# A recurrent layer on one core: one product cut into four column tiles, and three conv parts moved past a stage's end

## The chip, the cores and the metric

The kernel runs on one core of a Trainium2 chip. The metric is the device time of one execution in microseconds (us), as the median of several runs. The core's engines work in parallel, each through its own queue in order: TensorE (PE; its weight loads are shown apart as PEld), VectorE (DVE), ScalarE (ACT), GpSimd (POOL) and SyncE (SP), which issues the transfers here. They wait for each other through semaphores.

## The reference

The input `x` has 16 rows of 256 x 512 fp32 values; the condition has 512 values per row. Four layers follow each other, each added to `x`:

```python
x = x + _L0_cond_ref(x, cond_2048, L0_cond_Wq, L0_cond_Wo)          # masked self-attention
x = x + _L1_cond_ref(x, cond_2048[:, None, :])                      # causal conv, 16 taps, over the 256 positions
x = x + _L2_cond_ref(cond_2048, x, L2_cond_W_ih, L2_cond_W_hh, L2_cond_b_ih, L2_cond_b_hh)   # GRU over 256 steps
x = x + _L3_cond_ref(x, cond_2048, L3_cond_Wq, L3_cond_Wk, L3_cond_Wv, L3_cond_b)            # masked attention
```

The third layer is the one that the change touches. Its cell, run over 256 steps for 16 rows with a state of 512 values:

```python
gi = x @ W_ih + b_ih
gh = h @ W_hh + b_hh
r = sigmoid(i_r + h_r); z = sigmoid(i_z + h_z); n = tanh(i_n + r * h_n)
h_new = (1.0 - z) * n + z * h
```

## The kernel before

The kernel has three stages. The first (to about 667 us) computes the first attention for one row after another, in an order that a planner works out from durations and due times; its path for these inputs is `attend0_together`. As soon as a row is ready in `xT` (features on partitions), `early` (L537) makes the conv's first four parts of 16 positions for that row: on VectorE a product of a sliding view with the taps (L546), a sum over the taps (L547) and an addition of `x` (L548), three operations for each part, after one POOL copy of 64 positions into the small tile `early` (L540). The parts land in `yw[0]` (parts 1 and 2) and `yw[1]` (parts 3 and 4). There is a third such tile, `yw[2]`, made for the recurrence; the first thing written into it is a conv of step 0.

The second stage (to about 1796 us) is the recurrence. Here the order of every engine's work is written out by hand. The 16 rows stand as the 32 columns of a stationary operand (two steps' worth), and weights stream past. Each product's output is cut into four column tiles: four matmuls of 32 stationary columns each, that write 32 output partitions each (`state_part`, L1064, for the state's parts of r, n and z; `input_part`, L1043, for the inputs' parts of r and z). The inputs' part of n is made otherwise, by `turned_part` (L1051): weights are stationary, 128 columns of them in one matmul, and 16 steps of inputs (256 columns) stream past. It takes 16 such matmuls for the 16 steps of a part p; the recurrence does one in each step, for the part that follows, and every fourth one is followed by a ScalarE operation (L1062) that adds the bias and moves the result from PSUM into `turned`.

A step (`step`, L1078) is a loop through three engines. PE does r, n and z with the state; ScalarE takes the sigmoid of r (L1092); VectorE transposes r and n (L1093, L1095), multiplies and adds (L1096, L1097); ScalarE takes the tanh (L1099); VectorE transposes z (L1100), ScalarE its sigmoid (L1101), and VectorE ends with `d`, `m` and the new state, written to `hist` (L1102 to L1104). The next step's r needs that state. Behind each step, the loop body puts, in this order: input parts of a later step on PE; on odd steps three ScalarE copies of the biases (L1136); one `turned_part`; in some steps a ScalarE copy of conv results (`take`, L1035); and two pieces of VectorE work, conv operations (L528) or additions of the state to `xT` (`add_part`, L1071). The product with `turned_part` is in steps 0 to 239; steps 240 to 255 have none, and steps 254 and 255 have no input parts either.

Ahead of step 0 stand: ScalarE's loading of its function table (L1113), products that place the biases in PSUM (L1116), their copies (L1118), `take` for part 0, all input parts of the first two steps, and the 16 matmuls of `turned_part` for part 0. Before them in the program, outside of the order by hand, two POOL memsets clear `hist` and VectorE copies the condition into it as the first state (L1017 to L1019). The third stage is the second attention.

Of the kernel before, what the change touches and what calls it, by code (L numbers as in the profile page):

```python
# [15 lines left out]
P = 128  # L16
NEG = -1e30
B, D, T = 16, 256, 512
# [7 lines left out]
TAPS = 16  # L26
WIN = 32
PART = 16
EARLY = 4
# [231 lines left out]
def tile_kernel(ctx: ExitStack, tc: tile.TileContext, x, cond, Wq0, Wo0, W_ih, W_hh, b_ih, b_hh,  # L261
                Wq3, Wk3, Wv3, b3, consts, out, cols):
    nc = tc.nc
    inp = x
    KC = D // P
    NT = T // P
# [12 lines left out]
    condT = cpool.tile([P, NT, B], F32, tag="condT", name="condT")  # L279
# [7 lines left out]
    xT = cpool.tile([P, NT, B, D], F32, tag="xT", name="xT")  # L287
# [5 lines left out]
    yw = [ypool.tile([P, NT, B, WIN], F32, tag=f"yw{i}", name=f"yw{i}") for i in range(2)]  # L293
# [6 lines left out]
    wih = cpool.tile([P, NT, 3 * T], F32, tag="wih", name="wih")  # L300
# [236 lines left out]
    def early(b, w, xs, products):  # L537

        if w == 0:
            yield "POOL", 0.7, lambda: nc.gpsimd.tensor_copy(xs[:, :, TAPS - 1 :], xT[:, :, b, 0 : EARLY * PART])  # L540
        a = xs[:, :, w * PART : w * PART + TAPS].unsqueeze(2).broadcast_to([P, NT, PART, TAPS])
        steps = [list(d) for d in a.ap]
        steps[2][0] = 1
        every = bass.AP(tensor=a.tensor, offset=a.offset, ap=steps)
        y = yw[w // 2][:, :, b, w % 2 * PART : (w % 2 + 1) * PART]
        yield "DVE", 1.3, lambda: nc.vector.tensor_tensor(products, every, condT.unsqueeze(2).broadcast_to([P, NT, PART, TAPS]), ALU.mult)  # L546
        yield "DVE", 1.3, lambda: nc.vector.tensor_reduce(y, products, AX.X, ALU.add)  # L547
        yield "DVE", 0.2, lambda: nc.vector.tensor_tensor(y, y, xs[:, :, TAPS - 1 + w * PART : TAPS - 1 + (w + 1) * PART], ALU.add)  # L548
# [5 lines left out]
    with tc.tile_pool(name="setup0", bufs=1) as sp, tc.tile_pool(name="psetup0", bufs=2, space=PSUM) as pss:  # L554
# [23 lines left out]
        ps = pss.tile([P, T], F32, tag="psm", name="pgood")  # L578
# [3 lines left out]
        for j in range(NT):  # L582
            ps = pss.tile([P, T], F32, tag="psm", name=f"condT{j}")
# [4 lines left out]
        ps = pss.tile([P, T], F32, tag="psm", name="places")  # L588
# [27 lines left out]
    def attend0_all():  # L616
        with ExitStack() as es:
# [55 lines left out]
            def finish0(b, j):  # L673
                ps = at.small(f"po0_{b}_{j}")
                for g in range(at.G):
                    nc.tensor.matmul(ps[:, 0:D], lhsT=at.avs[b * at.G + g][:, j * P : (j + 1) * P], rhs=woP[:, g, :],
                                     start=(g == 0), stop=False)
                for dc in range(KC):
                    nc.tensor.matmul(ps[:, dc * P : (dc + 1) * P], lhsT=xs[b][:, dc, j * P : (j + 1) * P], rhs=ident,
                                     start=False, stop=(dc == KC - 1))  # L680
                nc.scalar.copy(xT[:, j, b], ps[:, 0:D])
                if j == NT - 1:
                    for w in range(EARLY):
                        for _, _, f in early(b, w, *tiles):
                            f()

# [20 lines left out]
    def attend0_together():  # L707
# [7 lines left out]
        with ExitStack() as es:  # L715
# [202 lines left out]
            def finish(b, g0, x, cx, done):  # L918

                oc, gt, po = ocs.new(), gts.new(), pss.new()  # L920
                n = plan.add("SP", 3.0, g0 + 0.3, [pss.take(po)], lambda: nc.sync.dma_start(
                    out=PO[po.i], in_=places_dram[b : b + 1, :].broadcast_to([P, T])))
                for c in range(NK):
                    n = plan.add("DVE", 0.6, g0 + 0.6, [n] + ([gts.take(gt)] if c == 0 else []), lambda c=c: nc.vector.tensor_scalar(
                        GT[gt.i][:, c], PO[po.i], cst("place")[:, c : c + 1], None, ALU.is_equal))
                pss.free(po, n)
                made = []
                for part in range(2):
                    sm = banks.new()

                    def product(part=part, sm=sm):
                        for c in range(2) if part == 0 else [2]:
                            r = P if c < 2 else TAILK + 1
                            for g in range(GQ):
                                nc.tensor.matmul(SM[0:r, sm.i][:, (c % 2) * D : (c % 2 + 1) * D], lhsT=CX[cx.i][:, g, c * P : c * P + r],
                                                 rhs=woT[:, g, :], start=(g == 0), stop=(g == GQ - 1))
                    m = plan.add("PE", 1.72 if part == 0 else 0.87, g0 + 2.2 + 0.05 * part, done + [banks.take(sm)] + ([] if part else [ocs.take(oc)]) + made, product)
                    c = plan.add("ACT", 0.62 if part == 0 else 0.4, g0 + 2.2, [m], lambda part=part, sm=sm: nc.scalar.copy(
                        OC[oc.i][:, 0:2].rearrange("p c d -> p (c d)") if part == 0 else OC[oc.i][0 : TAILK + 1, 2],
                        SM[0 : P if part == 0 else TAILK + 1, sm.i][:, 0 : (2 - part) * D]))  # L940
                    banks.free(sm, c)
                    made.append(c)
                cs.free(cx, m)
                outs, moved = [], []
                for half in range(2):
                    sm = banks.new()

                    def product(half=half, sm=sm):
                        for tj in range(2 * half, 2 * half + 2):
                            dst = SM[:, sm.i][:, (tj % 2) * D : (tj % 2 + 1) * D]  # L950
                            for c in range(NK):
                                r = P if c < 2 else TAILK + 1
                                nc.tensor.matmul(dst, lhsT=GT[gt.i][0:r, c, tj * P : (tj + 1) * P], rhs=OC[oc.i][0:r, c], start=(c == 0), stop=False)  # L953
                            for dc in range(KC):
                                nc.tensor.matmul(dst[:, dc * P : (dc + 1) * P], lhsT=X[x.i][:, dc, tj * P : (tj + 1) * P], rhs=ident,
                                                 start=False, stop=(dc == KC - 1))
                    m = plan.add("PE", 3.45, g0 + 2.4 + 0.05 * half, made + [n, banks.take(sm)] + moved, product)
                    moved.append(m)
                    outs.append(plan.add("ACT", 0.65, g0 + 2.4, [m], lambda half=half, sm=sm: nc.scalar.copy(
                        xT[:, 2 * half : 2 * half + 2, b], SM[:, sm.i].rearrange("p (c d) -> p c d", d=D))))  # L960
                    banks.free(sm, outs[-1])
                ocs.free(oc, *moved)
                gts.free(gt, *moved)
                xs_.free(x, *moved)
                ea, n = ears.new(), None
                for w in range(EARLY):
                    for engine, dur, f in early(b, w, *ear):
                        n = plan.add(engine, dur, g0 + 3.2 + 0.3 * w, [n] if n else outs + [ears.take(ea)], f)
                ears.free(ea, n)
# [37 lines left out]
    with ExitStack() as es:  # L1007
# [6 lines left out]


        hist = [gw.tile([P, PART, NT, 2 * B], F32, tag=f"hist{i}", name=f"hist{i}") for i in range(2)]
        for t in hist:  # L1017
            nc.gpsimd.memset(t, 0.0)
        nc.vector.tensor_copy(hist[1][:, PART - 1, :, 0:B], condT)  # L1019

        def state(t):

# [28 lines left out]
        def turned_part(p, q):  # L1051

            fo, kc = divmod(q, NT)
            if q == 0:
                turned[p] = gp.tile([P, NT, PART, B], F32, tag="turned", name=f"turned_{p}")
            if kc == 0:
                turned["ps"] = psw.tile([P, T], F32, tag="psm", name=f"pt_{p}_{fo}")
            ps = turned["ps"][:, 0 : PART * B]
            nc.tensor.matmul(ps, lhsT=wih[:, kc, 2 * T + fo * P : 2 * T + (fo + 1) * P],  # L1059
                             rhs=parts[p][:, kc].rearrange("p s b -> p (s b)"), start=(kc == 0), stop=(kc == NT - 1))  # L1060
            if kc == NT - 1:
                nc.scalar.activation(turned[p][:, fo].rearrange("p s b -> p (s b)"), ps, AF.Identity, bias=nbias[:, fo : fo + 1])  # L1062

# [44 lines left out]

        taps = [(f, k, w * WIN) for w in range(EARLY // 2, D // WIN) for f in range(NT) for k in range(TAPS)]
        parts, turned, added = {}, {}, 0  # L1110
        with tc.manual_schedule(engines=ENG):

            nc.scalar.activation(gp.tile([P, NT], F32, tag="table", name="table", bufs=1), nbias, AF.Sigmoid)  # L1113
            for k in range(2):
                for ps, base in zip(sets[k], (0, 32, 64)):
                    nc.tensor.matmul(ps, lhsT=cst("gsel")[base : base + 8], rhs=gbias[base : base + 8], start=True, stop=True)  # L1116
# [425 lines left out]
```

## Time and profile before

| what | us |
|---|---|
| median of three runs (2829.16 to 2835.69) | 2830.13 |
| the profiled execution's own time | 2828.66 |
| its span, from the first instruction to the last | 2826.9 |
| TensorE busy in it | 2747.6 |
| VectorE busy in it | 1845.0 |
| ScalarE busy in it | 1026.1 |
| GpSimd busy in it | 229.4 |

A reader of such a page should keep apart how long an engine is busy and how much of the end it decides. The page's groups give, for each line of the program, an operation with its shapes, how often it came, its total busy time and the mean length of one in ns, and then the idle time of its engine just before. The timeline gives single instructions (or runs of like ones) with start and length in us. A matmul's end is modelled and overlaps the next one's start, so for TensorE the distance from one start of weight loads to the next is the better measure. One fp32 matmul of the program shows as two records on PE and two on PEld.

### The profile page before, as it was taken

Reading aid. Unit: us, or ns where it says so; the run is one execution under the profiler, and the core shown is the slowest. Engines: PE = TensorE matmul, PEld = TensorE weight load, DVE = VectorE, ACT = ScalarE, POOL = GpSimd, SP = SyncE. Lnnn points to the kernel's source line nnn. Section 1 sums busy time; section 2 is a strip of 40 time slices with the busy share of each in tenths; the row PEclk is TensorE's granted clock in tenths of the full one; section 3 lists DMA queues with packets and bytes.
Section 4 is the critical chain, followed back from the end, with each engine's and each line's share of the span. In section 5 each row is a group of like instructions: output and inputs, shape, how many; then the busy total and the mean of one; then the engine's idle time right before and its main releaser. Section 6 shows DMA issues by size and latency. Waiting matters only on the chain.

```text
span 2826.9 us, 99913 instructions
## 1 busy us (share of the span) xinstructions
PE 2747.6 (97%) x45574; PEld 1833.1 (65%) x45574; DVE 1845.0 (65%) x3929; ACT 1026.1 (36%) x2360; POOL 229.4 (8%) x282
## 2 busy tenths in 40 slices
PE   8999999997999999999999999799999999999998
PEld 5666666665888888888888888544444444444442
DVE  3666766675788888888888655565555556555553
ACT  2333333332333333333333332144444444444444
POOL 1010001000000000000000000002111111121112
PEclk9999999998999999999999999999999999999998
DMA  1000000002000000000000000000000000000000
GB/s 61 23 24 12 23 23 24 22 10 99 4 4 4 4 4 4 4 4 4 4 4 4 4 4 4 2 1 12 13 8 8 8 9 8 9 16 8 9 9 17
DMA packets 15370, 36.79 MB, mean 13 GB/s; under 512 B 2084, under 2 KB 3364, under 8 KB 14804
## 3 DMA queue, kind: packets, MB, share of 16 engines
q1 hardware_dynamic: 14932, 30.24, 3.1%
q8 instruction: 361, 5.91, 0.9%
q14 instruction: 77, 0.63, 0.1%
HBM read 21.78 MB, written 8.45 MB: 11 GB/s over the span
## 4 chain that ended last, share of the span: by engine, by line
PE 95%; DVE 3%; ACT 1%; issue 1%; POOL 0%; DMA 0%; SPq 0%; DVEq 0%; ACTq 0%; POOLq 0%
PE pr L1068 9%; PE pn L1068 8%; PE pz L1068 8%; PE sC L1426 7%; PE sC L1380 6%; PE pt L1059 6%; PE avC L1440 5%; PE smA L875 4%; PE smA L901 4%; PE pz L1048 4%; PE pr L1048 4%; PE smC L1346 4%; PE smA L953 3%; PE smC L1288 3%; PE smA L794 3%; PE sC L1386 2%
## 5 line engine op out<-in xcount | busy, mean ns | idle before, releaser
L1395 DVE TENSOR_REDUCE nmC<-sC 128x4 f32<-128x1024 f32 x256 | 301.8, 1221 | 215.5 <-PE sC L1380 209.2
L1433 ACT ACTIVATE wih<-sC 128x1024 f32<-128x1024 f32 x320 | 310.2, 1023 | 177.9 <-PE sC L1426 176.7
L1068 PE MATMUL pr<-whh,hist 128*32 128x128 f32 x8192 | 279.1, 276 | 9.1 <-DVE hist L1104 9.1
L528 DVE SCALAR_TENSOR_TENSOR yw<-xT,condT,yw 128x512 f32<-128x512 f32 x360 | 269.5, 749 | 6.8
L1068 PE MATMUL pn<-whh,hist 128*32 128x128 f32 x8192 | 272.3, 273 | 0.0
L1068 PE MATMUL pz<-whh,hist 128*32 128x128 f32 x8192 | 271.8, 273 | 0.0
L1068 PEld LDWEIGHTS pr<-whh,hist 128*32 128x32 f32 x8192 | 209.5, 110 | 93.7 <-DVE hist L1104 42.3
L1068 PEld LDWEIGHTS pn<-whh,hist 128*32 128x32 f32 x8192 | 230.7, 110 | 0.1
L1068 PEld LDWEIGHTS pz<-whh,hist 128*32 128x32 f32 x8192 | 230.1, 110 | 0.0
L1048 PE MATMUL pr<-wih,xw 128*32 128x128 f32 x4096 | 209.7, 274 | 13.3 <-ACT xw L1041 13.2
L1426 PE MATMUL sC<-qC,kC 32*128 32x512 f32 (+1 forms) x1280 | 219.2, 637 | 0.6 <-ACT wih L1433 0.3
L1048 PE MATMUL pz<-wih,xw 128*32 128x128 f32 x4096 | 210.5, 274 | 0.3 <-issue 0.3
L848 DVE TENSOR_REDUCE whh<-smA 128x2 f32<-128x640 f32 (+1 forms) x192 | 148.9, 817 | 89.4 <-PE smA L840 81.0
L1099 ACT ACTIVATE nn<-pre 128x64 f32<-128x64 f32 x256 | 65.8, 257 | 383.2 <-DVE pre L1097 383.2
L1092 ACT ACTIVATE r<-pr 128x128 f32<-128x128 f32 x256 | 71.1, 278 | 334.7 <-PE pr L1068 334.7
L1059 PE MATMUL pt<-xw,wih 128*128 128x256 f32 x512 | 174.9, 428 | 0.0
L1093 DVE STREAM_TRANSPOSE rT<-r 128x128 f32<-128x128 f32 x256 | 79.7, 311 | 145.7 <-ACT r L1092 145.3
L1380 PE MATMUL sC<-kC,qC 32*128 32x256 f32 x2048 | 171.2, 400 | 0.4 <-DVE nmC L1395 0.3
L1380 PEld LDWEIGHTS sC<-kC,qC 32*128 32x128 f32 x2048 | 117.1, 184 | 55.9 <-issue 34.2
L1480 POOL TENSOR_TENSOR aC<-aC,pbC 128x512 f32<-128x512 f32 x64 | 81.5, 1280 | 853.1 <-ACT pbC L1478 853.0
L1440 PE MATMUL avC<-wih,whh 128*32 128x512 f32 x1024 | 137.0, 604 | 0.0
L1048 PEld LDWEIGHTS pr<-wih,xw 128*32 128x32 f32 x4096 | 126.0, 110 | 14.0 <-issue 13.7
(178 smaller groups left out, 4117.7 us busy)
## 6 DMA issues: line engine op xcount, KB each, us to landing
xA<-in_x_dram SPq DMA_DIRECT2D x16, 512.0 KB, 3.7
out_dram<-oC SPq DMA_DIRECT2D x32, 256.0 KB, 2.0
poA<-places SPq DMA_DIRECT2D x16, 256.0 KB, 3.7
wih<-in_L_cond_W_ih_dram SPq DMA_DIRECT2D x4, 768.0 KB, 6.2
whh<-in_L_cond_W_hh_dram SPq DMA_DIRECT2D x4, 768.0 KB, 5.3
C<-in_consts_dram SPq DMA_DIRECT2D x1, 1032.5 KB, 5.1
C<-in_consts_dram SPq DMA_DIRECT2D x1, 482.5 KB
wq0nat<-in_L_cond_Wq_dram SPq DMA_DIRECT2D x1, 256.0 KB, 3.7
```

The source lines that it names most:

```text
L528: nc.vector.scalar_tensor_tensor(acc, xT[:, f, :, lo : lo + WIN], condT[:, f, k : k + 1], xT[:, f, :, t0 : t0 + WIN] if k == 0 else acc, A ...
L848: nc.vector.tensor_reduce(dst[:, lo : lo + len(some)], SM[0:n, some[0] : some[-1] + 1, 0:ROOM], AX.X, ALU.max, negate=True)
L875: nc.tensor.matmul(SM[:, st[j].i, 0:ROOM], lhsT=left, rhs=Q[q.i][r] if own else NR[nr.i][r], start=own, stop=not own)
L901: nc.tensor.matmul(SM[r, to.i, 0:ROOM], lhsT=left, rhs=e[:, j], start=(kc == 0), stop=(kc == NK - 1))
L1048: nc.tensor.matmul(sets[k % 2][0 if g == GATE_R else 2][32 * j : 32 * j + 32].rearrange("p (f i) -> p f i", i=32), lhsT=x2, rhs=gates(wih, ...
L1059: nc.tensor.matmul(ps, lhsT=wih[:, kc, 2 * T + fo * P : 2 * T + (fo + 1) * P], rhs=parts[p][:, kc].rearrange("p s b -> p (s b)"), start=(k ...
L1068: nc.tensor.matmul(ps[32 * j : 32 * j + 32].rearrange("p (f i) -> p f i", i=32), lhsT=slot[:, f], rhs=gates(whh, f, j)[:, g], start=False, ...
L1380: nc.tensor.matmul(S[st[j // 2].i][:, j % 2, u * 2 * P : (u + 1) * 2 * P], lhsT=Q[qt.i][R * j : R * j + R, c : c + P], rhs=K[kt.i][R * j : ...
L1395: nc.vector.tensor_reduce(dst[:, :, :, e_at + 1], S[st[jp].i].rearrange("p j (u k) -> p j u k", u=2), AX.X, ALU.max, negate=True)
L1426: nc.tensor.matmul(S[st[j // 2].i][:, j % 2, :], lhsT=K[kt.i][r, kc * P : kc * P + P] if kc < 2 else K[kt.i][r, ROOM:], rhs=Q[qt.i][r, :], ...
L1433: lambda jp=jp, st=st, e=e: nc.scalar.activation(E[e.i][:, 2 * jp : 2 * jp + 2], S[st[jp].i], AF.Exp))
L1440: nc.tensor.matmul(AV[acc.i][R * j : R * j + R, :], lhsT=V[v.i][:, kc, 8 * (g // 2) + 2 * j + q], rhs=E[e.i][:, j], start=(kc == 0), stop= ...
```

## The change

The change does two things.

First, `turned_part` makes four matmuls in place of one: each has 32 of the 128 weight columns as its stationary operand and writes 32 of the 128 output partitions, while the same 256 columns of inputs stream past. The values are the same.

Second, for the last of the 16 rows, the first stage makes only the first of the four conv parts. Parts 2 to 4 are made at the head of the recurrence, by the same operations, with a POOL copy of their own. Their working space (the copy and the products) lies in `yw[2]`. The memsets of `hist` and the copy of the first state move behind them, into the order by hand.

```diff
@@ in attend0_all (not run for these inputs) and in finish of attend0_together
-                for w in range(EARLY):
+                for w in range(EARLY if b < B - 1 else 1):
@@
         hist = [gw.tile([P, PART, NT, 2 * B], F32, tag=f"hist{i}", name=f"hist{i}") for i in range(2)]
-        for t in hist:
-            nc.gpsimd.memset(t, 0.0)
-        nc.vector.tensor_copy(hist[1][:, PART - 1, :, 0:B], condT)
@@ in turned_part
-            nc.tensor.matmul(ps, lhsT=wih[:, kc, 2 * T + fo * P : 2 * T + (fo + 1) * P],
-                             rhs=parts[p][:, kc].rearrange("p s b -> p (s b)"), start=(kc == 0), stop=(kc == NT - 1))
+            for j in range(4):
+                nc.tensor.matmul(ps[32 * j : 32 * j + 32], lhsT=wih[:, kc, 2 * T + fo * P + 32 * j : 2 * T + fo * P + 32 * j + 32],
+                                 rhs=parts[p][:, kc].rearrange("p s b -> p (s b)"), start=(kc == 0), stop=(kc == NT - 1))
@@
         parts, turned, added = {}, {}, 0
+        n = TAPS - 1 + EARLY * PART
+        room = yw[2].rearrange("p f b s -> p (f b s)")
+        xs = room[:, 0 : NT * n].rearrange("p (f s) -> p f s", f=NT)
+        products = room[:, NT * n : NT * (n + PART * TAPS)].rearrange("p (f s k) -> p f s k", f=NT, k=TAPS)
         with tc.manual_schedule(engines=ENG):
             nc.scalar.activation(gp.tile([P, NT], F32, tag="table", name="table", bufs=1), nbias, AF.Sigmoid)
+            nc.gpsimd.tensor_copy(xs[:, :, TAPS - 1 :], xT[:, :, B - 1, 0 : EARLY * PART])
+            for w in range(1, EARLY):
+                for _, _, f in early(B - 1, w, xs, products):
+                    f()
+            for t in hist:
+                nc.gpsimd.memset(t, 0.0)
+            nc.vector.tensor_copy(hist[1][:, PART - 1, :, 0:B], condT)
             for k in range(2):
```

More of the change, by code (lines that the diff above doesn't have):

```diff
@@ L965, in finish @@
                 ea, n = ears.new(), None
-                for w in range(EARLY):
+                for w in range(EARLY if b < B - 1 else 1):
                     for engine, dur, f in early(b, w, *ear):
```

## The prediction

> **What bounds the kernel now.** I read the page first, for the share of each engine on the chain that ended last:
>
> ```profile
> PE 95%; DVE 3%; ACT 1%; issue 1%; POOL 0%; DMA 0%; SPq 0%; DVEq 0%; ACTq 0%; POOLq 0%
> ...
> L1059 PE MATMUL pt<-xw,wih 128*128 128x256 f32 x512 | 174.9, 428 | 0.0
> ```
>
> TensorE carries 95%, so the product of L1059 (256 in all, two records each: 16 ahead of the loop, one in each of steps 0 to 239) looks like 174.9 us of path. A share is no price, though: the loop closes on itself through VectorE and ScalarE, so I looked at the timeline of one step with the product and of the last full step, which has neither the product nor input parts.
>
> A step with the product (start, length, engine, line, idle before):
>
> ```profile
> 1725.01 0.81 PEld L1068 LDWEIGHTS pr<-whh,hist 128*32 128x32 f32 x32 [0.33 <-issue]
> ...
> 1728.20 0.24 PEld L1048 LDWEIGHTS pz<-wih,xw 128*32 128x32 f32 x8
> ...
> 1728.64 0.30 PEld L1059 LDWEIGHTS pt<-xw,wih 128*128 128x128 f32 x2 [0.20 <-issue]
> 1728.64 0.70 PE L1059 MATMUL pt<-xw,wih 128*128 128x256 f32 x2
> 1728.86 0.22 DVE L1104 TENSOR_TENSOR hist<-m,hist 128x64 f32<-128x64 f32 x1
> ...
> 1729.27 0.81 PEld L1068 LDWEIGHTS pr<-whh,hist 128*32 128x32 f32 x32 [0.33 <-DVE hist L1104]
> ```
>
> From r's first load to the next: 4.26 us, and PE is never free. Its parts: r, n and z take 0.79, 0.87 and 0.88 us to z's end at 1727.55, the four input parts run to 1728.44, then 0.20 of nothing, then the product. The new state is ready at 1729.08, yet r starts 0.19 later.
>
> The last full step:
>
> ```profile
> 1788.16 0.81 PEld L1068 LDWEIGHTS pr<-whh,hist 128*32 128x32 f32 x32 [0.67 <-DVE hist L1104]
> ...
> 1791.06 0.32 DVE L1100 STREAM_TRANSPOSE zT<-pz 128x128 f32<-128x128 f32 x1
> ...
> 1791.95 0.22 DVE L1104 TENSOR_TENSOR hist<-m,hist 128x64 f32<-128x64 f32 x1
> 1792.29 0.84 PEld L1068 LDWEIGHTS pr<-whh,hist 128*32 128x32 f32 x32 [1.57 <-ACT omz L1101]
> ```
>
> Weight loads idle for 1.57 us here, and the step still lasts 4.13. That is the floor: gates r, n, z one after another, then z's transpose, its sigmoid (1791.41, 0.26 us), two VectorE operations and back to PE. So the product costs little more than the idle time it fills.
>
> The second place is the entry to the recurrence, in the chain in order of time:
>
> ```profile
> 670.38 0.23 DVE yw L548
> ...
> 678.33 0.24 DVE yw L548
> 678.62 1.28 ACT L1113
> ...
> 681.24 0.66 PE pr L1048 x8
> ```
>
> Everything waits for VectorE's last conv parts of row 15.
>
> [...] 0.20 us before L1059's first load, 0.33 before r's, none between products of one mode. [...] Between 800 and 1100 us the queue view shows:
>
> ```profile
> q8 instruction: 72, 1.18, 1.6%
> ```
>
> 72 packets of 16.4 KB, [...] the share makes 1.6% x 16 x 300 / 72 = 1.07 us for one. [...]
>
> **The change, part by part.** *The product in four column tiles, in 240 steps.* Today PE spends from the end of the inputs' loads (1728.20 + 0.24 = 1728.44) to 1729.27 on it: 0.83 us[...]. [...] Its stream: 32 records of 128 columns in r, n or z take 0.87 us, 27 ns each; a record of 256 columns is taken at twice that, so 4 tiles x 2 records x 54 ns = 0.44 us, if the four run side by side as L1068's do. PE's sum falls from 4.26 to 4.26 - 0.83 + 0.44 = 3.87 us.
>
> But the floor stands. Steps 240 to 253 have the input parts and no product; r's loads begin at 1771.33, 1775.46 and 1779.62, two steps in 8.29 us: 4.145 each. So a step goes from PE's 4.26 to the loop's 4.145: 0.115 us gained, and PE idles 0.27. Late next is `hist` (L1104), behind z's transpose and sigmoid. The product could cost 0.71 us before PE were the bound again, so the unmeasured 0.44 hardly matters. Steps 0 and 8 do not gain (ScalarE's copies and the weight transposes set them): 238 x 0.115 = 27.4 us.
>
> Taken off: VectorE's filling between `hist` and rT. Two conv operations (1.53 us) leave 0.19 to 0.25 us before rT today, and r coming 0.07 to 0.12 sooner leaves some. The two additions of L1076 take 2.12 us from 774.67 and already push rT; they end too late for n's transpose by about 0.1 us once r comes sooner: 14 such steps, 1.4 us. ScalarE's fullest step (bias copies, `turned`, `take`) ends just before the next r: nothing. I take 26 us.
>
> Bound from the other side: from 1741.70 to 1792.29 twelve steps take 50.59 us, 4.216 each, as some show small "issue" gaps inside r. With those in every step the gain is measured against today's own mean, 400 us x 130 records / 12164 = 4.275: 0.06 x 238 = 14 us. I take the clean steps: [...]
>
> *In the prologue* the product's 16 repetitions take 7.31 us from 684.37 to 691.68; new 16 x 0.44 = 7.0: 0.3 gained.
>
> *Row 15's conv parts 2 to 4.* Nine VectorE operations (3 x 2.65 = 7.95 us) leave the end of the first stage. ScalarE's table load waits for VectorE's last operation there: 670.61 instead of 678.56, so table, bias copies, `take` and PE's inputs begin 7.95 earlier, at 673.3. The same nine run after a new POOL copy (0.40 us): 671.3 to 679.2, under PE's inputs (3.4 us) and products. Behind them on VectorE is only `hist`'s copy of the condition (0.2), which step 0's r needs: 679.5 against r at about 684. POOL's two memsets (3.55) stand behind its copy, and end at 674.8; were they held until VectorE is done, 682.8, still in time. `take(1)` now waits for part 2, done at 673.9, before ScalarE is there. Weights: `wih` is down before 664, the last `whh` piece lands at 672.0, both early enough. SP's load of wv3 comes earlier and is used in step 8. Region `yw2` is first written in step 0, behind these on VectorE. PE is at half clock here (granted 0.50 from about 671 to 684, with PE working from 681.2): an earlier start finds the same half clock for some 4 us, again the inputs, plus 0.4 us of product. Step 0's r: 691.68 to 684.0, gain 7.7 us with the 0.3 in it. If the cover failed altogether, it would be 0.
>
> **Sum.** 26 + 7.7 = 33.7 us; a few hundred instructions more to fetch and new alignments may take 1 to 2 back: 32. Against the profiled 2828.66 (span 2826.9 and 1.8 around it) that is 2796.7; the median of the runs shown is 1.5 above it, so 2798.
>
> **Rivals.** (1) *The steps gain nothing*: the loop is the bound already. For it: in the list of waits (696 to 1741 us) r's loads wait for `hist` in 113 steps, against 98 for "issue". Against: steps without the product are shorter. Only the prologue then: 2830 - 7.7 = 2822. (2) *The steps gain half*, with the gaps of the last block everywhere: 14 + 7.7, so 2808. (3) *Slower: PE starves for instructions.* A step's PE instructions rise from 260 to 272 (three more matmuls of four), 17.4 KB. If a block cannot come faster than the 300 / 72 = 4.17 us seen, a step takes 1.0625 x 4.17 = 4.43, 0.155 over today's mean: +37 - 8, so 2859. It decides from 4.06 us for a block (1.0625 x 4.06 = 4.31, where 0.032 x 240 has eaten the prologue's 7.7). Against: a fetch takes 1.07 us of the 4.17, so today's pace is what PE eats, not what the queue can bring. (4) *More than forecast*: if the loop's floor shrank too. Nothing in the trace offers it.
>
> **How the numbers follow.** Forecast 0.68 (2791 to 2804), half 0.16, nothing from the steps 0.06, slower 0.07, more 0.03. The range reaches over the second: 2790 to 2811. A difference of 0.3% (8.5 us) is about what a measurement of this kernel tells from none. Faster by more: 0.68 + 0.16 + 0.03 and part of the third, 0.89; within: 0.04; slower: 0.07.
>
> **What would show it.** Steps of 4.14 to 4.16 us with r's loads waiting for `hist` in nearly all of them; no gap before the product's loads; the product's eight records in 0.4 to 0.5 us; step 0's r at 684; ScalarE's table load at 670.7. Wrong, if steps stay at 4.26, if "issue" gaps grow, or if `hist`'s copy releases step 0.

## The result, and the profile after

| | before | after |
|---|---|---|
| median of six runs each | 2830.5 | 2805.6 |
| range of the runs | 2829.2 to 2835.7 | 2802.0 to 2808.4 |
| profiled execution's own time | 2828.7 | 2802.0 |
| its span | 2826.9 | 2800.2 |
| first weight load of step 0's r | 691.68 | 684.04 |
| recurrence, from the state of step 0 to that of step 255 | 1099.4 | 1079.6 |
| from there to the end | 1030.5 | 1030.9 |

The ratio is 0.9911 (0.9898 to 0.9923): 25 us faster, where 32 had been forecast. 2805.6 lies inside the range of 2790 to 2811, but just outside its main part (2791 to 2804), in the stretch that it reached over for the second rival (2808). In the profiled executions the 26.7 us of span come in two parts: 7.3 ahead of the state of step 0, and 19.8 in the recurrence; the rest gives back 0.4.

In the changed program the state's products stand in L1066, the inputs' parts in L1045, the product of `turned_part` in L1057, `take` in L1038, the sigmoid of r in L1090, the tanh in L1097, z's transpose and sigmoid in L1098 and L1099, `hist` in L1102, `add_part` in L1074, and the table load in L1116. From the page of after, the instruction queue, the shares of the chain, and two groups (busy us, mean ns of one, idle before and its main releaser):

```profile
q8 instruction: 373, 6.11, 0.9%
...
PE 94%; DVE 2%; ACT 1%; issue 1%; DMA 0%; POOL 0%; SPq 0%; DVEq 0%; ACTq 0%; POOLq 0%
...
L1066 PEld LDWEIGHTS pr<-whh,hist 128*32 128x32 f32 x8192 | 217.8, 110 | 119.8 <-DVE hist L1102 52.7
...
L1057 PE MATMUL pt<-xw,wih 128*32 128x256 f32 x2048 | 165.2, 380 | 0.2
```

The product's group has four times the records and 165.2 us for 174.9. This says nothing of its price, since they overlap: eight records of 380 ns each end within 0.61 us (the row at 1304.36 below). The chain's share of PE hardly moves (95% to 94%). What changed is seen in the timeline of two steps of after (start, length, engine, line):

```profile
1300.84 0.81 PEld L1066 LDWEIGHTS pr<-whh,hist 128*32 128x32 f32 x32 [0.47 <-DVE hist L1102]
...
1304.04 0.24 PEld L1045 LDWEIGHTS pz<-wih,xw 128*32 128x32 f32 x8
...
1304.26 0.24 PEld L1057 LDWEIGHTS pt<-xw,wih 128*32 128x32 f32 x8
1304.36 0.61 PE L1057 MATMUL pt<-xw,wih 128*32 128x256 f32 x8
...
1304.64 0.23 DVE L1102 TENSOR_TENSOR hist<-m,hist 128x64 f32<-128x64 f32 x1
...
1304.98 0.84 PEld L1066 LDWEIGHTS pr<-whh,hist 128*32 128x32 f32 x32 [0.49 <-issue]
```

The product's loads follow the inputs' at once. TensorE is through with loading at 1304.50 and idles until the state is there (0.47 and 0.49 in brackets). From r to r it is 4.14 us here. The waits of the loads between 690 and 1735 us (total, times, longest), first before, then after:

```profile
PEld pt L1059 <- issue: 47.9, 239, 0.6
PEld pr L1068 <- DVE hist L1104: 37.2, 112, 0.3
PEld pr L1068 <- issue: 33.0, 99, 0.5
PEld pr L1068 <- ACT xw L1041: 9.3, 28, 0.3
```

```profile
PEld pr L1066 <- DVE hist L1102: 49.7, 107, 0.7
PEld pr L1066 <- issue: 42.9, 95, 0.8
PEld pr L1066 <- ACT xw L1038: 13.6, 28, 0.5
PEld pz L1045 <- issue: 5.9, 12, 0.9
PEld pr L1045 <- issue: 3.6, 9, 0.6
```

The 47.9 us ahead of the product are gone. Two things are left to explain: why only half of r's waits name `hist`, and what the new waits for "issue" in the middle of the inputs' parts are. Both turned out to be one thing, which the experiments below show.

The median distance from one state to the next tells two kinds of step apart: 4.20 us in even and 4.32 in odd steps before, 4.08 and 4.22 after. On top of these, some steps are longer. I sum this excess over steps 1 to 240 where it is more than 0.03 us, without step 9, which has the weight transposes of step 8 behind it: 4.5 us in 21 steps before, 10.5 in 37 after (two expectations below have 9.5 for the latter, which is a little too low). After, the long steps come in groups about 15 steps apart (around 28, 42, 58, 74, 87, 104, 121 and so on), before in groups some 57 apart. One such group of after, weight loads only:

```profile
936.88 0.26 PEld L1045 LDWEIGHTS pz<-wih,xw 128*32 128x32 f32 x7
938.08 0.11 PEld L1045 LDWEIGHTS pz<-wih,xw 128*32 128x32 f32 x1 [0.94 <-issue]
...
942.10 0.11 PEld L1045 LDWEIGHTS pr<-wih,xw 128*32 128x32 f32 x1 [0.38 <-issue]
...
947.04 0.11 PEld L1066 LDWEIGHTS pz<-whh,hist 128*32 128x32 f32 x1 [1.30 <-issue]
```

The gap wanders backwards through the program: behind the 15th load of the four input groups, then behind the seventh, then ahead of the last load of z's state part. That is 8 loads a step, and with two loads and two matmuls for each fp32 matmul (the product's 1024 matmuls show as 2048 records of each), 16 instructions. In this form a step has 272 and, in odd steps, one semaphore instruction; 272.5 - 256 = 16.5. So these gaps sit at a border that comes every 256 instructions, and return after 256 / 16.5 = 15.5 steps. Before, 260.5 instructions gave 256 / 4.5 = 57 steps. The queue view shows the same unit: between 700 and 1700 us TensorE has 64244 records of loads and matmuls in after and 60183 in before, and q8 brings 251 and 235 packets of 16.4 KB, so 256.0 and 256.1 records for each. That is what a block means here, in the prediction and in what was expected of the runs.

The trace's own records bear it out. I count TensorE's records from its branch ahead of the recurrence and look at steps 10 to 240 of after. Besides the waits for the state and the product's own regular spacing, 31 gaps of more than 0.15 us are left, and all stand at one place of 256 (105 records behind the branch, or 105 and a multiple of 256). The border comes there 245 times, so one in eight is late. The packets of TensorE's instruction queue (q8) have times too: ahead of 30 of the 31 gaps' ends (the other stands at a semaphore instruction) the last packet had ended 1.20 to 1.58 us before. At the borders without a gap the median is 2.2 us, though 32 of 207 are as short. So the late instructions are among those whose block has only just come; that they waited for it is inferred from these times.

At the entry to the recurrence, after (its timeline):

```profile
670.61 0.23 DVE L548 TENSOR_TENSOR yw<-yw,early 128x64 f32<-128x64 f32 x1
...
670.90 1.28 ACT L1116 ACT_TABLE_LOAD   x1 [3.36 <-DMA whh<-in_L_cond_W_hh_dram]
671.04 0.40 POOL L1117 COPY yw<-xT 128x256 f32<-128x256 f32 x1 [2.98 <-DMA whh<-in_L_cond_W_hh_dram]
...
673.49 0.23 PEld L1045 LDWEIGHTS pr<-wih,xw 128*32 128x32 f32 x8 [5.36 <-issue]
...
674.14 1.23 DVE L546 TENSOR_TENSOR yw<-yw,condT 128x1024 f32<-128x1024 f32 x1 [3.31 <-ACT xw L1038]
...
682.10 0.19 DVE L1123 COPY hist<-condT 128x64 f32<-128x64 f32 x1
...
684.04 1.00 PEld L1066 LDWEIGHTS pr<-whh,hist 128*32 128x32 f32 x32
```

The table load comes at 670.90 (forecast 670.7) and r of step 0 at 684.04 (forecast 684.0). VectorE's moved parts begin 2.8 us later than forecast, at 674.14, and the state's copy is done at 682.29, still 1.75 ahead of r.

### The profile page after: what moved, and what is told of

It reads as the page before. It is cut to its first block, busy times and chain, and to the rows that moved or that the text cites. A ratio compares the mean times of both kernels' runs of the same rounds, so it can differ in the third digit from the quotient of the medians.

```text
span 2800.2 us, 102986 instructions
## 1 busy us (share of the span) xinstructions
PE 2718.1 (97%) x47110; PEld 1820.5 (65%) x47110; DVE 1844.1 (66%) x3929; ACT 1025.8 (37%) x2360; POOL 229.2 (8%) x283
## 4 chain that ended last, share of the span: by engine, by line
PE 94%; DVE 2%; ACT 1%; issue 1%; DMA 0%; POOL 0%; SPq 0%; DVEq 0%; ACTq 0%; POOLq 0%
PE pr L1066 10%; PE pn L1066 8%; PE pz L1066 8%; PE sC L1436 7%; PE sC L1390 6%; PE avC L1450 5%; PE smA L875 4%; PE pt L1057 4%; PE smA L901 4%; PE pr L1045 4%; PE pz L1045 4%; PE smC L1356 4%; PE smA L953 3%; PE smC L1298 3%; PE smA L794 3%; PE sC L1396 2%
## 5 line engine op out<-in xcount | busy, mean ns | idle before, releaser
L1066 PEld LDWEIGHTS pr<-whh,hist 128*32 128x32 f32 x8192 | 217.8, 110 | 119.8 <-DVE hist L1102 52.7
L1066 PE MATMUL pr<-whh,hist 128*32 128x128 f32 x8192 | 281.8, 276 | 13.5 <-DVE hist L1102 9.5
L1066 PE MATMUL pz<-whh,hist 128*32 128x128 f32 x8192 | 278.5, 273 | 1.5 <-issue 1.5
L1066 PE MATMUL pn<-whh,hist 128*32 128x128 f32 x8192 | 278.5, 273 | 0.0
L1066 PEld LDWEIGHTS pz<-whh,hist 128*32 128x32 f32 x8192 | 236.5, 110 | 2.2 <-issue 2.1
L1066 PEld LDWEIGHTS pn<-whh,hist 128*32 128x32 f32 x8192 | 236.7, 110 | 0.1
L1045 PE MATMUL pr<-wih,xw 128*32 128x128 f32 x4096 | 221.5, 274 | 6.7 <-ACT xw L1038 5.2
L1045 PE MATMUL pz<-wih,xw 128*32 128x128 f32 x4096 | 222.8, 274 | 2.6 <-issue 2.3
L1097 ACT ACTIVATE nn<-pre 128x64 f32<-128x64 f32 x256 | 65.7, 257 | 383.6 <-DVE pre L1095 383.6
L1090 ACT ACTIVATE r<-pr 128x128 f32<-128x128 f32 x256 | 70.9, 277 | 318.1 <-PE pr L1066 317.5
L1057 PE MATMUL pt<-xw,wih 128*32 128x256 f32 x2048 | 165.2, 380 | 0.2
L1045 PEld LDWEIGHTS pr<-wih,xw 128*32 128x32 f32 x4096 | 137.6, 110 | 9.5 <-issue 9.0
L1045 PEld LDWEIGHTS pz<-wih,xw 128*32 128x32 f32 x4096 | 138.8, 110 | 6.1 <-issue 5.9
## 6 DMA issues: line engine op xcount, KB each, us to landing
out_dram<-oC SPq DMA_DIRECT2D x32, 256.0 KB, 2.0
poA<-places SPq DMA_DIRECT2D x16, 256.0 KB, 3.9
wq0nat<-in_L_cond_Wq_dram SPq DMA_DIRECT2D x1, 256.0 KB, 3.8
```

Source lines behind the costliest of these rows:

```text
L1045: nc.tensor.matmul(sets[k % 2][0 if g == GATE_R else 2][32 * j : 32 * j + 32].rearrange("p (f i) -> p f i", i=32), lhsT=x2, rhs=gates(wih, ...
L1057: nc.tensor.matmul(ps[32 * j : 32 * j + 32], lhsT=wih[:, kc, 2 * T + fo * P + 32 * j : 2 * T + fo * P + 32 * j + 32], rhs=parts[p][:, kc]. ...
L1066: nc.tensor.matmul(ps[32 * j : 32 * j + 32].rearrange("p (f i) -> p f i", i=32), lhsT=slot[:, f], rhs=gates(whh, f, j)[:, g], start=False, ...
```

## The experiments

In all of them the kernel before ran beside on the same chip; ratios are against it.

**The two parts alone.** e1 is before with the four column tiles only, e2 is after with the old product.

```diff
# e1: before, with in turned_part
-            nc.tensor.matmul(ps, lhsT=wih[:, kc, 2 * T + fo * P : 2 * T + (fo + 1) * P], ...
+            for j in range(4):
+                nc.tensor.matmul(ps[32 * j : 32 * j + 32], lhsT=wih[:, kc, 2 * T + fo * P + 32 * j : ...
# e2: after, with the same lines the other way round
```

> Only the four column tiles; row 15's conv parts stay at the end of the first stage. Clean steps of 4.145 us as in the changed kernel, and the lost steps that it showed (see below). My theory (the loop is the floor, what is lost beyond it are waits for PE's instruction blocks): 18 to 20 us faster than the kernel before, about 2811. Rival (the moved conv parts cause the lost time by disturbing the first steps): the steps alone bring the whole 26 us, about 2804.

> Only the moved conv parts; the product stays one matmul of 128 columns. My theory: step 0's r 7.5 to 8 us sooner, steps of 4.26 us unchanged, so about 2822.5. Rival (they disturb later work): less than 6 us gained.

e1: 2813.7 us, ratio 0.9947 (0.9930 to 0.9963); steps of 4.08 and 4.22, an excess of 14.5 us in 48 steps, groups every 15 to 16 steps, r of step 0 at 691.75. e2: 2824.2, ratio 0.9976 (0.9968 to 0.9985); r of step 0 at 684.5, steps as before. So the tiles bring 17 us (18 to 20 had been expected) and the moved parts 7, together 24 of the 25 measured. Within the noise the parts do not help or hinder each other.

**Where the groups of long steps come from.** e3 puts 32 small matmuls (128 instructions) ahead of the loop; they write the same bias values once more. If the groups belong to a border every 256 instructions, they have to shift by half their distance. If they belong to certain steps (the 16-step parts of `take` and `turned`), they stay.

```diff
+            for _ in range(32):
+                nc.tensor.matmul(sets[1][1], lhsT=cst("gsel")[32:40], rhs=gbias[32:40], start=True, stop=True)
             for i, ps in enumerate(sets[0]):
```

> The changed kernel with 32 more small matmuls ahead of the loop, while PE idles (they write the same bias values again): 128 more instructions, half a block of 256. Theory (late instruction blocks): a step of the changed kernel has 272.5 instructions on average, so a block's end comes 16.5 instructions earlier in each step and the lost steps return every 256 / 16.5 = 15.5 steps; half a block more moves all of them by 7.75 steps, from about t = 58, 74, 104, 121, 136 to about t = 51, 66, 96, 113, 128 (or 8 later), at the same total loss. Rival (collisions on ScalarE or VectorE, whose work repeats every 16 steps): the lost steps stay where they are. Time 2800 to 2808 under both.

The groups moved to around steps 20, 36, 52, 66, 82, 98, 112, 129 and 144, seven or eight away from those of after, and their 37 gaps stand at the same place of 256. The rhythm of the 16-step parts is out as their cause. The time, 2817.7 us (ratio 0.9956, 0.9939 to 0.9972), isn't that of the groups: it was expected at 2800 to 2808. The 32 matmuls, 64 records, took 11.3 us ahead of step 0 (r at 691.0), the excess was 14.8, and the third stage took 5 us longer (1035.8, as later in e7, which also has 128 instructions more), for which I have no cause.

e4 has more instructions in a step: the product in halves of 128 columns, four more matmuls, 288.5 instructions. The border then returns after 256 / 32.5 = 8 steps.

```diff
-            for j in range(4):
-                nc.tensor.matmul(ps[32 * j : 32 * j + 32], ..., rhs=parts[p][:, kc].rearrange("p s b -> p (s b)"), ...
+            for h in range(2):
+                for j in range(4):
+                    nc.tensor.matmul(ps[32 * j : 32 * j + 32, 128 * h : 128 * h + 128], ...,
+                                     rhs=parts[p][:, kc, 8 * h : 8 * h + 8].rearrange("p s b -> p (s b)"), ...
```

> The changed kernel with each column tile's product cut once more, into two halves of 128 streamed columns: same values and the same stream, but 288.5 instructions a step. Theory (late blocks): lost steps return every 256 / 32.5 = 7.9 steps, some 30 places in 240 steps, each shorter; total loss 8 to 14 us against the changed kernel's 9.5. Rival (collisions in the loop's own 16-step pattern): the pattern of lost steps does not change. If PE were the bound anywhere, the eight more records a step would show as steps over 4.15 throughout.

The groups came every 8 steps (30, 38, 46, 54 and on), with 29.1 us of excess in 89 steps, two to almost four times the loss expected; undisturbed steps kept 4.08 and 4.21. 2819.4 us, ratio 0.9961 (0.9952 to 0.9970). The rule of 256 held: 67 gaps, all at the place of after. The loss grows much faster than the number of borders (260 for 245).

**Exactly 256 instructions.** If a border can be late only in some places, a step of exactly 256 instructions holds it in one place for good, and that place can be chosen. e5 to e8 merge r's and z's input parts of every other quarter of the features into one matmul of twice the columns, which puts both gates into one PSUM tile; 0, 16, 32 or 48 small matmuls ahead of the loop move the border by 0, 64, 128 or 192 instructions.

```diff
-        sets = [[psg.tile([P, P], F32, tag=f"{n}{i}", name=f"p{n}{i}") for n in "rnz"] for i in range(2)]
+        both = [psg.tile([P, 2, P], F32, tag=f"rz{i}", name=f"prz{i}") for i in range(2)]
+        sets = [[both[i][:, 0], psg.tile([P, P], F32, tag=f"n{i}", name=f"pn{i}"), both[i][:, 1]] for i in range(2)]
... (z's bias rows get a tile of their own)
+        def inputs(k, f):
+            if f % 2:
+                for g in (GATE_R, GATE_Z):
+                    input_part(k, f, g)
+                return
...
+            for j in range(4):
+                nc.tensor.matmul(both[k % 2][32 * j : 32 * j + 32].rearrange("p g (f i) -> p g f i", i=32),
+                                 lhsT=x2, rhs=gates(wih, f, j)[:, 0:2], start=False, stop=False, skip_group_check=True)
... (e6 to e8 alone; 16, 32 or 48 times)
+            spare = psw.tile([P, T], F32, tag="psm", name="spare")
+            for _ in range(16):
+                nc.tensor.matmul(spare[0:32, 0:16], lhsT=cst("gsel")[0:8, 0:32], rhs=gbias[0:8, 0:16], start=True, stop=True)
```

> The changed kernel with exactly 256 instructions a step: for every second block of 128 features the inputs' parts of r and z are made by one matmul of 256 streamed columns into one PSUM tile, in place of two of 128 (64 matmuls a step, not 68; same values, same stream). Theory (late blocks): a block's end stands at the same place of every step from step 9 to 239, so either every second step or so loses something (8 to 40 us in all) or none does (under 2 us); the 15.5-step pattern is gone in any case. At a good place: 2796 to 2798. Rival (collisions on VectorE or ScalarE with a 16-step pattern): the changed kernel's 9.5 us and its pattern stay, about 2805.

> As e5, with 16 small matmuls more ahead of the loop (64 instructions, a quarter of a block; they write a tile that nothing reads). Theory: the block's end stands at another quarter of the step; of the four places of e5 to e8 one or two lose, the others do not, and between best and worst lie more than 6 us. Rival: all four alike within 3 us.

> As e6 with 128 instructions more than e5, half a block. Theory and rival as for e6.

> As e6 with 192 instructions more than e5, three quarters of a block. Theory and rival as for e6; the 48 small matmuls may end after PE's idle time and put step 0 off by 1 to 2 us.

| | us | ratio | excess to step 240 |
|---|---|---|---|
| e5 | 2778.1 | 0.9814 (0.9797 to 0.9830) | 1.3 |
| e6 | 2778.1 | 0.9812 (0.9796 to 0.9829) | 1.2 |
| e7 | 2776.8 | 0.9808 (0.9791 to 0.9824) | 1.3 |
| e8 | 2780.8 | 0.9821 (0.9805 to 0.9838) | 1.3 |

All four lay some 20 us below what I had expected, and no place was a bad one. What excess is left is not of blocks: in e5, 14 of its 15 steps are every sixteenth one, those with the two additions of `add_part`. The excess explains 9.2 us of the difference to after; the rest is that every step now takes 4.08 us, the odd ones too. My picture of the odd steps had been wrong: I had taken 4.145, the mean of 4.08 and 4.22, for the floor of the loop.

What is longer in an odd step of after? Medians over undisturbed steps from 100 to 235, in us after the end of the state before:

| | even step | odd step | e5, both |
|---|---|---|---|
| first load of r | 0.053 | 0.116 | 0.053 |
| sigmoid of r begins | 1.203 | 1.284 | 1.203 |
| `pre` begins | 2.689 | 2.768 | 2.688 |
| tanh begins | 2.948 | 3.087 | 2.946 |
| tanh ends | 3.204 | 3.344 | 3.203 |
| z's transpose ends | 3.267 | 3.350 | 3.267 |
| z's sigmoid begins | 3.300 | 3.444 | 3.300 |
| next state written | 4.075 | 4.217 | 4.074 |

The odd step loses 0.08 up to r's sigmoid, keeps that up to the end of z's transpose, and loses 0.06 more at z's sigmoid, which begins 0.094 us behind the transpose in place of 0.033. The tanh is late by the same 0.06, but it ends before z's transpose does, and so isn't what z's sigmoid waits for (e11 below sets the two clearly apart). The trace holds what stands there, though the views leave it out. A step pair shares the tile `pr`; in the odd step r's first matmul must wait for VectorE's `hist` and also for ScalarE, which has read the same `pr` in the step before. In this trace only semaphore instructions carry more than one wait (232 of them carry two, every other instruction at most one), and a separate one (an EventSemaphore) stands ahead of r: in the step at 1304.98 it waits for VectorE, and r's first load behind it for ScalarE. Of steps 100 to 234, all 67 odd ones have it and no even one. ScalarE has two of its own in the same 67 steps, ahead of the tanh and ahead of z's sigmoid. In e5 the shared tile makes z's first matmul wait for ScalarE's reading of r, long before the next r, which then needs only `hist` (253 waits for it between 690 and 1735 us, 112.7 us in all); no such instruction is left on TensorE in the steps, and none on ScalarE ahead of the tanh or of z's sigmoid. e5 had changed three things at once: the count, the merging and this wait.

**Count, merging or the second wait.** e9 takes only the shared tile and leaves the matmuls as in after (272 instructions); e10 merges the input parts of all four quarters (240).

```diff
# e9 and e10: tiles as in e5; in place of its function inputs
+        def inputs(k, f):                       # e9
+            for g in (GATE_R, GATE_Z):
+                input_part(k, f, g)
...
+        def inputs(k, f):                       # e10
+            xw, s0 = parts[2 * k // PART], 2 * k % PART
+            x2 = xw[:, f, s0 : s0 + 2].rearrange("p s b -> p (s b)")
+            for j in range(4):
+                nc.tensor.matmul(both[k % 2][32 * j : 32 * j + 32].rearrange("p g (f i) -> p g f i", i=32), ...
```

> The changed kernel with r and z of a pair of steps in one PSUM tile, matmuls unmerged: TensorE has 68 fp32 matmuls (272 instructions) a step as in the changed kernel, but no separate semaphore instruction ahead of r in the odd steps. Theory A (the extra 0.14 us of each odd step, 4.22 for 4.08, is that second wait and what follows from it; late blocks are a matter of 272 against 256 instructions): both kinds of step at 4.08 (119 x 0.14 = 17 us gained), late blocks stay, in groups every 16 steps, about 10 us in all: 2788 (2784 to 2794). Theory B (the steps of the four kernels before got shorter by the merged matmuls): odd steps stay at 4.22, 2803 to 2807. Theory C (the odd step's semaphore instruction is what makes blocks late): no groups, 2777.

> As the kernels with 256 instructions, but the r and z inputs of all four f merged, not of two: 60 fp32 matmuls, 240 instructions a step. Both kinds of step at 4.08, since the chain and not TensorE sets them. Theory A (a block is late where its 256 instructions hold none of TensorE's waits for hist, so that they are used up in 3.6 us; a block of more than one step always holds one): no late blocks though the boundary moves by 16 instructions a step: 2777 (2774 to 2781), the same as with 256. Theory B (a boundary that falls among the products behind the state's matmuls is late, whatever the block holds): groups of late blocks every 16 steps, 8 to 12 us: 2785 to 2789. Theory C (TensorE's work still sets the step): 16 fewer instructions make it faster, 2760 to 2770.

e9: 2776.5 us, ratio 0.9817 (0.9802 to 0.9832). e10: 2776.5, ratio 0.9815 (0.9800 to 0.9831). In both, all steps take 4.075 us. Of e9's theories A, which I held, fell, and C is right: with 272 instructions a step the border still passes through the whole step every 16 steps, but the excess is 1.9 us instead of 10.5, and 2 of 245 borders have a gap. Of e10's theories, B and C fell. Theory A named the right time, but its reason does not carry: in e9 the wait for `hist` comes every 272 instructions, so some blocks of 256 hold none there too, and no groups of late ones follow. e9's waits of the loads, same window as above:

```profile
PEld prz L1074 <- DVE hist L1110: 109.5, 250, 0.8
```

and its steps:

```profile
1302.57 0.23 DVE L1110 TENSOR_TENSOR hist<-m,hist 128x64 f32<-128x64 f32 x1
...
1302.85 0.81 PEld L1074 LDWEIGHTS prz<-whh,hist 128*32 128x32 f32 x32 [0.42 <-DVE hist L1110]
...
1306.64 0.22 DVE L1110 TENSOR_TENSOR hist<-m,hist 128x64 f32<-128x64 f32 x1
...
1306.92 0.81 PEld L1074 LDWEIGHTS prz<-whh,hist 128*32 128x32 f32 x32 [0.42 <-DVE hist L1110]
```

One line has taken the place of three: r waits for `hist` in every step. The 95 waits for "issue" and 28 for "ACT xw" of after, 123 together, were all in odd steps, and the 107 for `hist` all in even ones. The instruction that waited for `hist` there was the semaphore instruction, which the profile doesn't count as work, so that r itself seemed to wait for nothing, or for whatever ended last.

**Without sharing a tile.** e9 also changed where z lies. e11 keeps after's tiles and puts one small matmul that reads r ahead of z, so that TensorE has waited for ScalarE early; e12 does the same to before. The small matmul's result goes to two unused columns.

```diff
             nc.vector.tensor_tensor(pre, rn, turned[t // PART][:, :, t % PART], ALU.add)
+            nc.tensor.matmul(looks[t // 2 % 2], lhsT=r[:, 0:32], rhs=r[:, 0:2], start=False, stop=True, skip_group_check=True)
             state_part(slot, pz, GATE_Z)
```

> The changed kernel with its separate PSUM tiles, plus one small matmul ahead of z in each step that reads r (its result goes to two unused columns). TensorE has then waited for ScalarE's r a step before it would have to ahead of the next r, so the separate semaphore instruction of the odd steps goes, with no tile shared; 69 matmuls, 276 instructions a step. Theory A (the semaphore instruction ahead of r is the cause both of the 4.22 and of the late blocks): both kinds of step at 4.08, or up to 0.03 more for the added matmul's two loads, excess of late blocks under 2 us: 2776 to 2785. Theory B (sharing a tile is what helped): odd steps stay at 4.22 or more, groups stay, 2805 to 2812.

> The kernel before (its product in one 128x256 matmul, first conv parts in SyncE's old place) with the same small matmul ahead of z, so that the semaphore instruction of the odd steps goes: 66 matmuls, 264 instructions a step. In before, r begins 0.18 us after hist in an even step, set by TensorE's own work [...], and an odd step is 4.32 against 4.20. Theory A: odd steps fall to 4.20, or 4.23 with the added matmul in both, 0.09 to 0.12 x 119 = 11 to 14 us, and the 4 us of late blocks go: 2812 to 2818. Theory B (TensorE's work sets the odd steps of before too, the semaphore instruction costs nothing there): 2828 to 2834, the added matmul's 0.03 x 238 = 7 us on top at worst.

e11: 2801.2 us, ratio 0.9894 (0.9879 to 0.9909), outside both expectations. Its waits, and three rows of one step:

```profile
PEld pr L1068 <- DVE hist L1105: 119.1, 247, 0.7
```

```profile
1302.01 0.22 PEld L1098 LDWEIGHTS pz<-r 128*32 128x32 f32 x2
...
1303.30 0.32 DVE L1101 STREAM_TRANSPOSE zT<-pz 128x128 f32<-128x128 f32 x1
...
1303.65 0.26 ACT L1102 ACTIVATE omz<-zT 128x64 f32<-128x64 f32 x1 [0.16 <-DVE zT L1101]
```

The semaphore instruction is gone: r begins 0.053 after the state in both kinds of step, and over the even and odd medians (4.14 and 4.20) only 0.7 us of excess is left. So both effects on TensorE hang on that instruction and not on the shared tile. That the time is not better has two reasons. The small matmul stands ahead of z, and z is on the loop's path: its transpose comes 0.062 later in every step (3.013 for 2.951 after the state). And ScalarE's own semaphore instructions are still there in odd steps. The one that counts stands ahead of z's sigmoid: z's transpose ends at 3.330 in both kinds of step, the sigmoid begins at 3.363 in even and 3.423 in odd ones. (The tanh is 0.062 late as well, but ends at 3.262, long enough before.) 4.075 + 0.062 + 0.060 is the 4.20 measured. I had overlooked the second and taken too little for the first.

e12: 2842.1 us, ratio 1.0040 (1.0026 to 1.0053), slower. Its waits:

```profile
PEld pr L1070 <- DVE hist L1107: 79.1, 238, 0.4
PEld pt L1061 <- issue: 47.4, 239, 0.2
```

The semaphore instruction is gone here too, and the excess is 0.4 us, but steps take 4.24 and 4.36, a mean of 4.30 for 4.26, and the wait ahead of the old product stands as in before. In before TensorE's own work set the step: there the odd steps' second wait cost nothing, and the small matmul's 0.04 was paid in full. Theory B was right, and even its upper end, 2834, was too low.

| kernel | semaphore instruction in odd steps (PE) | instructions a step | even, odd step | excess |
|---|---|---|---|---|
| before | yes | 260.5 | 4.20, 4.32 | 4.5 |
| e12 | no | 264 | 4.24, 4.36 | 0.4 |
| after | yes | 272.5 | 4.08, 4.22 | 10.5 |
| e4 | yes | 288.5 | 4.08, 4.21 | 29.1 |
| e11 | no | 276 | 4.14, 4.20 | 0.7 |
| e9 | no | 272 | 4.08, 4.08 | 1.9 |
| e5 to e8 | no | 256 | 4.08, 4.08 | 1.2 to 1.3 |
| e10 | no | 240 | 4.08, 4.08 | 1.3 |

e9 and e10 are the best of these versions, 27 to 29 us below after (by the ratios and by the medians); e9 needs no more than the one tile for r and z, with z's bias rows in a tile of their own.

What stays open is why the semaphore instruction makes blocks late. The trace of after has two more signs of it in the odd steps: r starts 0.063 us later (0.116 for 0.053), and the loads run some 1% slower (2.478 us for 2.449 over the state's 96 records). What TensorE does while it waits there, no run shows.

## Why the prediction was right, and where it was not

- *TensorE's work sets the step before, the loop's floor after*: right. The gap ahead of the product went, and r's loads now wait for the state (what the 0.20 and 0.33 consisted of, no run shows; that the new form would be rid of them I could only infer from the lack of such gaps between like products). e12 shows from the other side that TensorE set the step of before. 0.115 x 238 = 27.4 us was forecast; from the medians it is (4.202 + 4.319) / 2 - (4.075 + 4.217) / 2 = 0.1145, or 27.3.
- *The product at 0.44 us*: its loads span 1304.26 to 1304.50, and four matmuls side by side end 0.61 after their first start, by the modelled ends. Whether it is 0.44 or 0.6 made no difference, as forecast.
- *L1076's additions cost 1.4 us*: wrong. Those steps kept their length. In one, with the additions from 1304.79, rT came late, yet hT began at 1307.07, within 0.04 us of its place in other odd steps, and the next state was there 4.21 after the last.
- *The prologue at 7.7 us*: 7.6 at r of step 0 and 7.3 at its state. Right, with a miss of no consequence: VectorE's moved parts began 2.8 us later than I said, which their cover took.
- *One to two us for more instructions and new alignments*: this is the term that failed. The excess rose by 6.0 us, and step 9 took 1.0 more (15.05 for 14.01). I had taken the clean steps because with the product a bad phase should move on from step to step instead of staying, an estimate that nothing in the trace of before had shown. In after it does move on, but it comes by every 15.5 steps in place of every 57, and that count could have been made from the packets and records of before. 27.3 + 7.3 - 6.0 - 1.0 is 27.6, against 26.7 of span measured; 0.2 of the rest was lost in the last 15 steps and 0.4 behind them. The 1.4 us that I took off for the additions were not lost, which made up for part of this miss: that was luck.
- *Rival 2, half of the gain in the steps*: 2808, nearer to the measured 2805.6 than my 2798. Its mechanism, gaps for blocks, is what took back 6 us; its size, gaps as in the last block in every step (14 us left), did not come: the recurrence gained 19.8. My argument against it, that a bad phase moves on, was no ground to put the gaps at next to nothing.
- *Rival 3, starved for instructions*: it did not decide, but its mechanism is that of the lost 6 us, and e4 shows it growing, to 29.1. As the rival had it, a block was to take at least 4.17 us at all times (its 1.0625 is 272 / 256). In after 76 blocks came between 800 and 1100 us, one every 3.95 us, and e9 has the same 272 instructions a step at 4.075 us, with 1.9 us of excess in all, so the rate of the blocks is not the limit at 272 instructions.
- *Rival 4, a shorter floor, "Nothing in the trace offers it"*: wrong, in what it says of the trace. The change did not shorten the floor, but the trace of before offered it: r waited for "issue" in 98 steps and for `hist` in 113, and I used this only as an argument about TensorE. Half of a loop's steps waiting for "issue" in the same place meant a separate wait instruction there. 4.145 was the mean of two kinds of step, and 0.14 us of every odd one could be removed.

## What to carry to other kernels

When a loop's steps come in two lengths, look at the waits of the two apart before calling the mean a floor; here the 95 waits for "issue" ahead of r, which needs the last result, came from a second wait in an instruction of its own, and without it both kinds of step took 4.08 us for 4.08 and 4.22. Let the engine take the older of two waits earlier, at an instruction that is not on the path (a shared tile did it here for nothing, at 2776.5 us in e9; an added matmul on the path, e11, cost about as much as it won, at 2801.2 for 2805.6). And count an engine's instructions per step against 256 where it has such waits: in before, after and e4 (260.5, 272.5 and 288.5) the remainder gave the distance at which late blocks returned, 57, 15.5 and 8 steps.

## What the runs showed of the hardware that I had not expected

- A semaphore instruction ahead of TensorE's r cost 0.08 us in each step that had it, and brought late steps of up to 1.4 us; ScalarE's ahead of z's sigmoid cost 0.06. In before, with TensorE as the bound, the steps were no shorter without it (e12: 4.24 and 4.36 for 4.20 and 4.32).
- Without that instruction, programs of 240, 256, 272 and 276 TensorE instructions a step ran with 0.7 to 1.9 us of late steps in a millisecond.
- Between the first stage and the recurrence each engine has a branch instruction. VectorE's ran at 670.62, its next instruction of any kind at 673.69, three microseconds later, though what VectorE needed last, GpSimd's copy, was done at 671.44. The semaphore instructions that stood there took 0.05 each, so they waited for nothing; the releaser that the 674.14 row names is the nearest event, not the cause. ScalarE's branch left a hole of the same length (666.96 to 669.96). Not every branch does: VectorE's next one, at 1769.29, left 0.05. GpSimd's 2.98 us of idle time (the 671.04 row) are another thing: its semaphore instruction waited for VectorE's last operation there. The trace gives the length of the two holes; what fills them it does not show.
